# Graph attention on one Trainium2 core: own chunks ahead of shared rows, scatters eight steps behind, no writes behind gathers, and a wait for the score product three chunks ahead

## The chip, the cores and the metric

The kernel runs on one core of a Trainium2 chip. A core has five engines that each work off their own queue in order: TensorE (PE, with its weight loads shown apart as PEld), VectorE (DVE), ScalarE (ACT), GpSimd (POOL) and SyncE (SP). They hand work to each other through semaphores. Sixteen DMA engines move data between the chip's memory and the core's SBUF; POOL, ACT and SP issue the transfers. The metric is the device time of one execution in microseconds. Before the change it is 3419.34 us, the median of three runs (3416.0 to 3419.94).

## What is computed

Two layers of graph attention on 6250 nodes and 100000 edges, with 128 features in 8 heads of 16. Nodes have one of 16 types, edges one of 32. The core of a layer in the reference:

```
k = typed_linear(x, ntype, Wk).reshape(n, H, HS)     # also q and v
kT = jnp.einsum('nhd,htdo->nhto', k, Watt)           # a key for each node and edge type
vT = jnp.einsum('nhd,htdo->nhto', v, Wmsg)           # a value for each node and edge type
a = jnp.einsum('ehd,ehd->eh', kT[src, :, etype], q[dst]) * pri[:, etype].T / SQRT_D
att = edge_softmax(a, dst, n)
hag = segment_sum(vT[src, :, etype] * att, dst)
h = silu(typed_linear(hag, ntype, Wa))
h = h * alpha + x * (1.0 - alpha)
return layernorm(h) * g + b
```

After two layers follow a linear map, a residual and a layer norm.

## The kernel before

**Tables.** For each layer a table in the chip's memory holds one row of 256 numbers (key and value) for each pair of node and edge type, 200000 rows. The table of layer 0 is made in a first stage. The table of layer 1 is made during layer 0: as soon as a group of nodes has its new features, `table_block` (line 262) multiplies them on PE, ACT copies the result from PSUM into a tile `st` of 2 MB (line 281), and POOL scatters the tile into the table (`scatter`, line 1555). There are three `st` buffers (`STB`, line 1063). A node block of 128 nodes gives two tiles, so 49 blocks give 98 scatters.

**Blocks, slots and chunks.** Nodes are sorted by type class and degree into 49 blocks of 128, one node to a partition. Block b has `KB[b]` slots, as many as its largest degree. For each slot POOL issues one indirect DMA (line 1324) that gathers 128 rows of the table, 128 KB. Slots go in chunks of `CH` = 4; a chunk shares one `kv` tile, of which there are 12. A layer has 819 gathers in 224 chunks. When a chunk's rows have landed, DVE multiplies the keys by the query (line 1344, the score product) and sums over each head (line 1350).

**The end of a block.** When all scores of a block are there, the generator `finished` (line 1189) runs, one step at a time, between the chunks of the next block: mask, maximum, exponential on ACT (line 1213), denominator (line 1219), then chunk by chunk the values are weighted (line 1247) and added up (line 1254), and summed (line 1257). A `kv` tile is free again after its weighting and adding. In layer 0 the sum `acc` is in SBUF, in layer 1 it is in PSUM, in the first half of the tile `pair`.

**Shared rows.** One block, `TOP`, holds nodes with up to 42 edges. It has 26 own slots and 2 shared rows: a node with more than 26 edges gets rows of other partitions, and `moved` (line 1180) carries scores and values between partitions by a PE product and an ACT copy. It is handled once per layer. Before the change, `finished` deals with the shared rows (lines 1221 to 1237) ahead of the own chunks (lines 1243 to 1256).

**What sets the order.** POOL's order is that of the program text. For the other engines a planner orders the instructions by the text's order and by when it expects them to be ready; so a changed wait or a removed instruction can change their order too. Node work (`nodes`, line 1426) and table pieces are spread over the chunks by `tick` (line 1140). A finished `st` tile is put on the list `late` with a count (line 1579), each step of the table work lowers the counts (`later`, line 1548), and at zero the scatter is issued. A layer-1 gather waits for all scatters.

**Writes behind gathers.** After every gather POOL writes two pieces of 32 numbers per partition into a tile `pause` that nobody reads (lines 1327 to 1330).

Of the kernel before, what the change touches and what calls it, by code (L numbers as in the profile page):

```python
# [9 lines left out]
F32 = mybir.dt.float32  # L10
BF16 = mybir.dt.bfloat16
I32 = mybir.dt.int32
AF = mybir.ActivationFunctionType
ALU = mybir.AluOpType
# [4 lines left out]
P = 128  # L19
# [6 lines left out]
SB = 4  # L26
# [4 lines left out]

CH = 4

PAUSES = 12


PIECE = 6
# [34 lines left out]
def kernel(  # L72
# [21 lines left out]
    nc = tc.nc  # L94
    N, D = out.shape
# [5 lines left out]
    _, H, RT, HS, _ = Watt.shape  # L101
# [250 lines left out]
    half = wide // 2  # L352
# [43 lines left out]
    for i0 in range(0, NT, 17):  # L396
        sl = slice(i0, min(i0 + 17, NT))
        k = sl.stop - sl.start
# [173 lines left out]
    with tc.If(unsorted > 0):  # L572
# [7 lines left out]
        with tc.For_i(0, EC, 1) as j:  # L580
            pair = pp.tile([P, 2], I32, name="pair")
# [476 lines left out]
    def arm(fast):  # L1058
# [5 lines left out]
        ep = ctx2.enter_context(tc.tile_pool(name="ep", bufs=2))  # L1064
# [62 lines left out]
        def edges(l):  # L1127
# [61 lines left out]
            def finished(s, i, chunks, kvt, a, pair, sums, den):  # L1189


                i0, k, _ = sbs[s]
                K = KB[i0 + i]
                av = a[:, :K, :]
                rest = None
                if i0 + i == TOP:
                    rest, chunks = kvt[-1], chunks[:-1]
                    moved(pair, node_of, rest[:, 3, :RK * REST * H],
                          a[:, OWN:K, :].rearrange("p k h -> p (k h)"))
                    yield  # L1200
                nc.vector.tensor_tensor(  # L1201
                    av, av, neg[:, NO[i0 + i]:NO[i0 + i] + K].unsqueeze(2)
                    .to_broadcast([P, K, H]), op=ALU.add)
                yield
                m = ep.tile([P, H], F32, name="m")
                nc.vector.tensor_reduce(m, av.rearrange("p k h -> p h k"), axis=AX.X, op=ALU.max)
                yield
                nc.vector.tensor_tensor(av, av, m.unsqueeze(1).to_broadcast([P, K, H]),  # L1208
                                        op=ALU.subtract)
                w = av  # L1210
                if l and rest is None:
                    w = pair[:, 1, D:D + K * H].rearrange("p (k h) -> p k h", h=H)
                nc.scalar.activation(w, av, AF.Exp)
                if rest is not None:
                    moved(pair, rows_of, a[:, OWN:K, :].rearrange("p k h -> p (k h)"),
                          rest[:, 3, :RK * REST * H])
                yield
                yield
                nc.vector.tensor_reduce(den[:, i, :], w.rearrange("p k h -> p h k"),
                                        axis=AX.X, op=ALU.add)  # L1220
                if rest is not None:

                    wk = rest[:, 3, :RK * REST * H].rearrange("p (r c) -> p r c", r=RK)
                    nc.vector.tensor_tensor(
                        wk, wk, nth.unsqueeze(2).to_broadcast([P, RK, REST * H]), op=ALU.mult)
                    wr = rest[:, 3, D:D + REST * H]
                    nc.vector.tensor_reduce(wr, wk.rearrange("p r c -> p c r"), axis=AX.X,
                                            op=ALU.add)
                    yield
                    v = rest[:, :REST, D:].rearrange("p k (h d) -> p k h d", h=H)  # L1230
                    nc.vector.tensor_tensor(
                        v, v, wr.rearrange("p (k h) -> p k h", h=H).unsqueeze(3)
                        .to_broadcast([P, REST, H, HS]), op=ALU.mult)
                    nc.vector.tensor_tensor(rest[:, 2, D:], rest[:, 0, D:], rest[:, 1, D:],
                                            op=ALU.add)
                    moved(pair, node_of, rest[:, 2, D:], rest[:, 2, :D])
                    yield

                if l == 0:
                    acc = ep.tile([P, CH, D], F32, name="acc", bufs=1)  # L1240
                else:
                    acc = pair[:, 0].rearrange("p (k c) -> p k c", k=CH)
                for j in range(len(chunks) + 1):
                    if j < len(chunks):
                        j0, j1 = chunks[j]
                        v = kvt[j][:, :j1 - j0, D:]
                        nc.vector.tensor_tensor(  # L1247
                            (v if j else acc).rearrange("p k (h d) -> p k h d", h=H),
                            v.rearrange("p k (h d) -> p k h d", h=H),
                            w[:, j0:j1, :].unsqueeze(3).to_broadcast([P, j1 - j0, H, HS]),  # L1250
                            op=ALU.mult)
                    if j > 1:
                        j0, j1 = chunks[j - 1]
                        nc.vector.tensor_tensor(acc[:, :j1 - j0], kvt[j - 1][:, :j1 - j0, D:],  # L1254
                                                acc[:, :j1 - j0], op=ALU.add)
                    yield
                nc.vector.tensor_reduce(sums[:, i, :], acc.rearrange("p k c -> p c k"),  # L1257
                                        axis=AX.X, op=ALU.add)
                if rest is not None:
                    nc.vector.tensor_tensor(sums[:, i, :], sums[:, i, :], rest[:, 2, :D],  # L1260
                                            op=ALU.add)
                if i == k - 1:
                    spread(work, nodes(l, *sbs[s], sums, den, *got[s][1:], lambda gen: table(s, gen)),
                           (36 if l else 27) + (len(sbs[s][2]) - TC) // 2 * (1 if l else 3),
                           pace(s + 1) * (1.0 if l or mixed(s) else 0.75))
# [17 lines left out]
                    tables[s] = gen  # L1283
                    spread(pieces, gen, 4, PIECE)

            pause = ep.tile([P, PAUSES, 2, SB * H], BF16, name="pause", bufs=1)
            before = iter(())
            q, pair = query(0, 0)
            for s, (i0, k, types) in enumerate(sbs):
# [7 lines left out]
                for i in range(k):  # L1297
                    b = i0 + i
# [3 lines left out]
                    chunks = [(j, min(j + CH, own)) for j in range(0, own, CH)]  # L1302
                    if b == TOP:
                        chunks.append((OWN, OWN + REST))
                    kvt = []
# [12 lines left out]
                    for j0, j1 in chunks:  # L1318
                        c = j1 - j0
                        kv = ep.tile([P, CH, 2 * D], F32, name="kv", bufs=12)  # L1320
                        kvt.append(kv)
                        for j in range(j0, j1):
                            at = KO[b] + j
                            get = nc.gpsimd.indirect_dma_start(  # L1324
                                out=kv[:, j - j0, :], out_offset=None, in_=tabs[l][:],
                                in_offset=bass.IndirectOffsetOnAxis(ap=ell[:, at:at + 1], axis=0))
                            if at % PAUSES == 0:
                                pause = ep.tile([P, PAUSES, 2, SB * H], BF16, name="pause", bufs=1)
                            for half in range(2):
                                nc.gpsimd.memset(pause[:, at % PAUSES, half], 0.0)  # L1330
                            if l == 1:
                                for put in puts:
                                    tc.add_manual_dep(
                                        get.ins, put.ins.name,
                                        mybir.DependencyInfo(mybir.DependencyClass.Sync,
                                                             mybir.DependencyReason.DATA),
                                        reason="rows of the table")
                                puts.clear()
                        kk = kv[:, :c, :D]
                        rest = b == TOP and j0 == OWN  # L1340
                        if rest:
                            moved(pair, rows_of, got[s][0][:, i, :], kv[:, 2, :D])
                        of = kv[:, 2, :D] if rest else q
                        nc.vector.tensor_tensor(  # L1344
                            kk, kk, of.unsqueeze(1).to_broadcast([P, c, D]), op=ALU.mult)
                        step()
                        tick(c / 3)
                        to = (kv[:, 3, D:D + c * H].rearrange("p (k h) -> p k h", h=H) if rest
# [3 lines left out]
                        if rest:  # L1352
# [4 lines left out]
                                op=ALU.mult)  # L1357
# [10 lines left out]
                    q, pair = then[0] if then else (None, None)  # L1368
# [177 lines left out]
        late = []  # L1546
# [21 lines left out]
        def pieces_of(i0, k, kT, vT, share):  # L1568

            def steps(gen):  # L1570

                for _ in gen:
                    for _ in range(2):
                        later()
                        yield

            for i in range(k):
                def store(tg, st, b=i0 + i):
                    late.append([5, (tg, st, b)])

                yield from steps(table_block(ep, tps, kT, vT, i, share, STB, store,
                                             2 if fast else 1))
            while late and not fast:
                later()
# [172 lines left out]
```

## Time and profile before

| | |
|---|---|
| median of the runs | 3419.34 us |
| the profiled execution | 3404.81 us |
| its span, first to last instruction | 3403.0 us |
| POOL busy | 2403.5 us, 71% |
| DVE busy | 1863.1 us, 55% |
| PE busy | 1674.7 us, 49% |
| ACT busy | 1035.7 us, 30% |
| mean DMA | 198 GB/s |

The profile is of one execution. It has stages: up to about 640 us the first table and the sorting, from 640 to 2045 us the gathers of layer 0 (with the making of table 1), to 2115 us the last scatters, to 3360 us the gathers of layer 1, and 43 us of an end. A share of busy time over the whole span is a mean over stages with different limits, so each stage is read by itself. In the timeline a row gives start, duration, engine, line, operation, what is written and read, and, in brackets, how long the engine was idle before and what ended that; "issue" means that no wait is seen.

### The profile page before, as it was taken

The page shows a single profiled execution, that of the slowest core. Times are in us where ns is not written, and L with a number is a line of the kernel's source. Part 1 is how long each engine was busy: PE and PEld are TensorE (multiplying, and loading weights), DVE is VectorE, ACT ScalarE, POOL GpSimd, SP SyncE. Part 2 cuts the span into 40 slices and gives each one's busy share as a digit, 9 for nine tenths or more (in the row PEclk, how much of TensorE's full clock was granted, in tenths as well). Part 3 has the DMA queues.
Part 4 walks back from the last instruction along what each step waited for, and adds up shares of the span by engine and source line. Part 5 has one row for each costly group of instructions (what it writes and reads, how often), then busy time and mean ns, then how long its engine had stood idle before and what let it go on. Part 6 is the DMA issues. An engine that isn't in the chain of part 4 may idle for free. (4 is left out here: it accounts for less than half of the span.)

```text
span 3403.0 us, 24779 instructions
## 1 busy us (share of the span) xinstructions
PE 1674.7 (49%) x5291; PEld 747.6 (22%) x5291; DVE 1863.1 (55%) x4307; ACT 1035.7 (30%) x1720; POOL 2403.5 (71%) x5400
## 2 busy tenths in 40 slices
PE   5899989403676757776686664011111132012112
PEld 2444434201232323232232222000100011001001
DVE  8626642156555576566565543456455565566554
ACT  2788755200334123423344443011100120012111
POOL 2233267588677886888878872888688788888884
PEclk8889876556677667887777776555555555555555
DMA  6899989833676466766677767333233333333331
GB/s 181 363 418 420 391 332 345 269 87 97 215 266 253 134 219 225 279 251 212 225 263 286 279 234 294 99 99 97 83 98 96 98 108 98 94 99 99 94 89 44
DMA packets 169096, 674.80 MB, mean 198 GB/s; under 512 B 52972, under 2 KB 83726, under 8 KB 143886
## 3 DMA queue, kind: packets, MB, share of 16 engines
q0 software_dynamic: 114144, 638.40, 52.5%
q1 hardware_dynamic: 38402, 27.55, 3.0%
q10 hardware_dynamic: 16384, 7.11, 0.9%
q14 instruction: 120, 0.98, 0.1%
q8 instruction: 46, 0.75, 0.1%
HBM read 248.64 MB, written 425.02 MB: 198 GB/s over the span
## 5 line engine op out<-in xcount | busy, mean ns | idle before, releaser
L1324 POOL DMA_INDIRECT kv<-tab,ell x1638 | 1647.1, 1006 | 358.8 <-issue 298.2
L281 ACT COPY st<-tb 128x512 f32<-128x512 f32 (+1 forms) x1108 | 744.3, 759 | 507.9 <-PE tb L274 296.7
L1344 DVE TENSOR_TENSOR kv<-kv,tb 128x512 f32<-128x512 f32 (+3 forms) x223 | 142.9, 641 | 480.5 <-DMA kv<-tab,ell 469.0
L259 PE MATMUL nb<-ident,hag 128*128 128x128 f32 x98 | 26.4, 408 | 744.6 <-DVE hag L1391 420.5
L1330 POOL MEMSET pause<- 128x32 bf16 x3276 | 336.5, 141 | 49.0 <-remote 28.1
L1024 POOL DMA_INDIRECT tab<-st,rows x98 | 100.7, 1028 | 279.4 <-ACT st L281 253.2
L274 PE MATMUL tb<-bdv,kvT 32*128 32x512 f32 x784 | 257.7, 787 | 64.1 <-ACT st L281 50.9
L274 PE MATMUL tb<-bdk,kvT 32*128 32x512 f32 x784 | 261.6, 814 | 48.7 <-ACT st L281 35.0
L1344 DVE TENSOR_TENSOR kv<-kv,q 128x512 f32<-128x512 f32 (+3 forms) x223 | 142.8, 643 | 260.0 <-DMA kv<-tab,ell 237.7
L1350 DVE TENSOR_REDUCE a<-kv 128x32 f32<-128x512 f32 (+2 forms) x446 | 282.1, 635 | 4.7 <-DVE a L1208 1.5
L274 PE MATMUL tb<-bdv,vT 32*128 32x512 f32 x784 | 276.3, 776 | 10.7 <-ACT st L281 7.9
L251 PE MATMUL nb<-xm,wa 128*128 128x512 f32 (+2 forms) x336 | 188.9, 721 | 130.9 <-DVE xm L237 79.9
L274 PE MATMUL tb<-bdk,kT 32*128 32x512 f32 x784 | 236.9, 795 | 5.0 <-DVE st L279 2.5
L237 DVE SCALAR_TENSOR_TENSOR xm<-ntb,nb 128x512 f32<-128x512 bf16 (+2 forms) x304 | 156.6, 562 | 144.0 <-remote 65.5
L1556 POOL DMA_INDIRECT tab<-st,row x98 | 106.7, 1089 | 167.6 <-ACT st L281 120.0
L259 PEld LDWEIGHTS nb<-ident,hag 128*128 128x128 f32 x98 | 16.0, 203 | 761.7 <-issue 564.4
L1503 PE MATMUL nb<-xm,wkqv 128*128 128x512 f32 (+2 forms) x312 | 148.6, 639 | 41.1 <-issue 23.4
L251 PE MATMUL nb<-xm,wq 128*128 128x384 f32 (+2 forms) x168 | 85.0, 655 | 153.1 <-DVE a L1201 91.3
L1177 ACT COPY tb<-hq 128x128 f32<-128x128 f32 x49 | 13.1, 269 | 478.7 <-DVE sums L1257 311.7
L259 PE MATMUL nb<-ident,hs 128*128 128x128 f32 x98 | 36.3, 457 | 208.6 <-DVE hs L1464 122.0
L251 PEld LDWEIGHTS nb<-xm,wa 128*128 128x128 f32 x336 | 87.4, 277 | 232.7 <-DVE xm L237 99.7
L274 PEld LDWEIGHTS tb<-bdv,vT 32*128 32x128 f32 x784 | 110.9, 219 | 117.6 <-ACT st L281 78.6
(337 smaller groups left out, 2742.7 us busy)
## 6 DMA issues: line engine op xcount, KB each, us to landing
kv<-tab,ell POOLq DMA_INDIRECT x1638
hr<-xrd SPq DMA_DIRECT2D x14, 256.0 KB
hqd<-hs SPq DMA_DIRECT2D x7, 512.0 KB
hq<-hqd SPq DMA_DIRECT2D x7, 512.0 KB
xrd<-xr POOLq DMA_DIRECT2D x10, 256.0 KB
hr<-xrd SPq DMA_DIRECT2D x10, 192.0 KB
hqd<-hs SPq DMA_DIRECT2D x5, 384.0 KB
hq<-hqd SPq DMA_DIRECT2D x5, 384.0 KB
```

The source lines that it names most:

```text
L237: nc.vector.scalar_tensor_tensor(xm[:, :n], ntb[:, :n], float(t), hT[:, :n], op0=ALU.is_equal, op1=ALU.mult)
L251: nc.tensor.matmul(ps[:, :n], w[:, t, :], xm[:, :n], start=(t == types[0]), stop=(t == types[-1]))
L259: nc.tensor.transpose(tr[:, i * P:(i + 1) * P], src_of(i), ident)
L274: nc.tensor.matmul(pt[:, b], yT[s, i * P:(i + 1) * P], bd[s, tt, :], start=True, stop=True)
L281: nc.scalar.copy(to, pt)
L1024: put = nc.gpsimd.indirect_dma_start(out=tabs[0].rearrange("(n t) c -> n (t c)", t=16), out_offset=bass.IndirectOffsetOnAxis(ap=rows1[:, t ...
L1324: get = nc.gpsimd.indirect_dma_start(out=kv[:, j - j0, :], out_offset=None, in_=tabs[l][:], in_offset=bass.IndirectOffsetOnAxis(ap=ell[:, ...
L1330: nc.gpsimd.memset(pause[:, at % PAUSES, half], 0.0)
L1344: nc.vector.tensor_tensor(kk, kk, of.unsqueeze(1).to_broadcast([P, c, D]), op=ALU.mult)
L1350: nc.vector.tensor_reduce(to, kk.rearrange("p k (h d) -> p k h d", h=H), axis=AX.X, op=ALU.add)
L1503: nc.tensor.matmul(ps[:, :n], wkqv[:, j, t, :], xm[:, :n], start=(t == types[0]), stop=(t == types[-1]))
L1556: put = nc.gpsimd.indirect_dma_start(out=tabs[1].rearrange("(n t) c -> n (t c)", t=16), out_offset=bass.IndirectOffsetOnAxis(ap=row2[:, tg ...
```

## The change

Four edits.

1. In `finished` the block of statements for the shared rows moves behind the loop over the own chunks. In layer 1 the block `TOP` then sums into an SBUF tile `acc` and no longer into PSUM.
2. The two `pause` writes behind each gather go.
3. The first gather of each chunk gets a wait: the score product of the chunk three before it, in the same layer, must be done (`AHEAD` = 3, `begun`).
4. A scatter is issued eight steps of the table work after its tile is complete and no longer five.

```diff
-PAUSES = 12
+AHEAD = 3
...
                 nc.vector.tensor_reduce(den[:, i, :], w.rearrange("p k h -> p h k"),
                                         axis=AX.X, op=ALU.add)
-                if rest is not None:
-
-                    wk = rest[:, 3, :RK * REST * H].rearrange("p (r c) -> p r c", r=RK)
...
-                    moved(pair, node_of, rest[:, 2, D:], rest[:, 2, :D])
-                    yield
-
-                if l == 0:
+                if l == 0 or rest is not None:
                     acc = ep.tile([P, CH, D], F32, name="acc", bufs=1)
                 else:
                     acc = pair[:, 0].rearrange("p (k c) -> p k c", k=CH)
...
                         nc.vector.tensor_tensor(acc[:, :j1 - j0], kvt[j - 1][:, :j1 - j0, D:],
                                                 acc[:, :j1 - j0], op=ALU.add)
                     yield
+                if rest is not None:
+
+                    wk = rest[:, 3, :RK * REST * H].rearrange("p (r c) -> p r c", r=RK)
+                    nc.vector.tensor_tensor(
+                        wk, wk, nth.unsqueeze(2).to_broadcast([P, RK, REST * H]), op=ALU.mult)
+                    wr = rest[:, 3, D:D + REST * H]
+                    nc.vector.tensor_reduce(wr, wk.rearrange("p r c -> p c r"), axis=AX.X,
+                                            op=ALU.add)
+                    yield
+                    v = rest[:, :REST, D:].rearrange("p k (h d) -> p k h d", h=H)
+                    nc.vector.tensor_tensor(
+                        v, v, wr.rearrange("p (k h) -> p k h", h=H).unsqueeze(3)
+                        .to_broadcast([P, REST, H, HS]), op=ALU.mult)
+                    nc.vector.tensor_tensor(rest[:, 2, D:], rest[:, 0, D:], rest[:, 1, D:],
+                                            op=ALU.add)
+                    moved(pair, node_of, rest[:, 2, D:], rest[:, 2, :D])
+                    yield
+
                 nc.vector.tensor_reduce(sums[:, i, :], acc.rearrange("p k c -> p c k"),
                                         axis=AX.X, op=ALU.add)
...
-            pause = ep.tile([P, PAUSES, 2, SB * H], BF16, name="pause", bufs=1)
+            begun = []
...
-                            if at % PAUSES == 0:
-                                pause = ep.tile([P, PAUSES, 2, SB * H], BF16, name="pause", bufs=1)
-                            for half in range(2):
-                                nc.gpsimd.memset(pause[:, at % PAUSES, half], 0.0)
+                            if j == j0 and len(begun) >= AHEAD:
+                                tc.add_manual_dep(
+                                    get.ins, begun[-AHEAD],
+                                    mybir.DependencyInfo(mybir.DependencyClass.Sync,
+                                                         mybir.DependencyReason.DATA),
+                                    reason="no further ahead of the scores")
...
-                        nc.vector.tensor_tensor(
-                            kk, kk, of.unsqueeze(1).to_broadcast([P, c, D]), op=ALU.mult)
+                        begun.append(nc.vector.tensor_tensor(
+                            kk, kk, of.unsqueeze(1).to_broadcast([P, c, D]), op=ALU.mult).ins.name)
...
                 def store(tg, st, b=i0 + i):
-                    late.append([5, (tg, st, b)])
+                    late.append([8, (tg, st, b)])
```

More of the change, by code (lines that the diff above doesn't have):

```diff
@@ L1220, in finished @@
                                         axis=AX.X, op=ALU.add)
-                if rest is not None:
-                    wk = rest[:, 3, :RK * REST * H].rearrange("p (r c) -> p r c", r=RK)
-                    nc.vector.tensor_tensor(
[L1225 to L1228, printed above, removed]
-                    yield
[L1230 to L1235, printed above, removed]
-                    moved(pair, node_of, rest[:, 2, D:], rest[:, 2, :D])
-                    yield
-                if l == 0:
+                if l == 0 or rest is not None:
                     acc = ep.tile([P, CH, D], F32, name="acc", bufs=1)
@@ L1343, in edges @@
                         of = kv[:, 2, :D] if rest else q
-                        nc.vector.tensor_tensor(
-                            kk, kk, of.unsqueeze(1).to_broadcast([P, c, D]), op=ALU.mult)
+                        begun.append(nc.vector.tensor_tensor(
+                            kk, kk, of.unsqueeze(1).to_broadcast([P, c, D]), op=ALU.mult).ins.name)
                         step()
```

## The prediction

> **What bounds the kernel now.** I read the table by stage first, then POOL's groups in the two gather stages, then the waits there, then the timeline at the places that the change touches. The rows by stage give the length, then busy time of PE, PEld, DVE, ACT and POOL, the granted clock, the DMA share and GB/s:
>
> ```profile
> 0.00:640.00 640.00, 552.66 (x2100) 260.53 (x2100) 321.33 (x797) 389.48 (x763) 267.15 (x339) 0.80 0.89 347
> 640.00:2045.00 1405.00, 869.04 (x2570) 357.54 (x2570) 799.14 (x1705) 470.72 (x625) 1124.22 (x2548) 0.71 0.63 221
> 2045.00:2115.00 70.00, 38.43 (x140) 18.31 (x140) 26.15 (x54) 24.55 (x31) 7.93 (x8) 0.70 0.79 317
> 2115.00:3360.00 1245.00, 204.75 (x457) 105.12 (x458) 696.37 (x1689) 141.96 (x287) 1000.21 (x2502) 0.54 0.33 97
> ```
>
> Layer 1 is POOL's stage: 1000 of 1245 us busy, PE at 205, DMA at a third. In layer 0 POOL has 1124 of 1405 us, but PE, at a clock of 0.71, has 869 and DVE 799, each in order. The groups of POOL, layer 0 then layer 1, with busy time, mean ns and idle time before:
>
> ```profile
> L1324 POOL DMA_INDIRECT kv<-tab,ell x819 | 860.0, 1050 | 163.9 <-issue 134.4 <-SPq L1753 14.7 <-DVE acc L1247 6.4
> L1330 POOL MEMSET pause<- 128x32 bf16 x1638 | 167.4, 142 | 3.4 <-remote 2.2 <-issue 0.5 <-POOL pause L1330 0.2
> L1556 POOL DMA_INDIRECT tab<-st,row x91 | 99.8, 1096 | 117.2 <-ACT st L281 89.5 <-issue 15.7 <-ACT a L1213 7.7
> ...
> L1324 POOL DMA_INDIRECT kv<-tab,ell x819 | 787.2, 961 | 194.9 <-issue 163.8 <-DVE tb L1247 19.2 <-DVE a L1350 1.0
> ```
>
> And who waits in layer 0, then in layer 1 (us in total, times, longest):
>
> ```profile
> DVE kv L1344 <- DMA kv<-tab,ell: 234.2, 80, 8.7
> POOL tab L1556 <- ACT st L281: 89.5, 20, 10.3
> ACT st L281 <- DMA tab<-st,row: 16.2, 5, 7.4
> ...
> DVE kv L1344 <- DMA kv<-tab,ell: 469.0, 157, 20.3
> POOL kv L1324 <- DVE tb L1247: 19.2, 1, 19.2
> ```
>
> In layer 1 DVE stands idle for rows 469 us and POOL for DVE hardly at all, so a quicker POOL is a shorter stage. In layer 0 DVE waits for rows 234 us and POOL waits for ACT 89.5 us: it is mixed.
>
> **The pause writes go.** 336 us of busy time are not 336 us of path, as the distance from one gather to the next shows, with the writes and (a loop without them, early in the kernel) without:
>
> ```profile
> 2629.62 0.95 POOL L1324 DMA_INDIRECT kv<-tab,ell  x1 [0.15 <-issue]
> 2630.57 0.21 POOL L1330 MEMSET pause<- 128x32 bf16 x2
> 2630.93 0.95 POOL L1324 DMA_INDIRECT kv<-tab,ell  x1 [0.15 <-issue]
> ...
> 44.24 0.95 POOL L968 DMA_INDIRECT xg<-in_x_dram,inv  x1 [0.30 <-issue]
> 45.49 0.95 POOL L968 DMA_INDIRECT xg<-in_x_dram,inv  x1 [0.30 <-issue]
> ```
>
> With them 1.31 us (0.95 + 0.21 + 0.15), without 1.25 (0.95 + 0.30): the writes fill a gap that is there anyway, and 0.06 us remains. 819 x 0.06 = 49 us per layer. In layer 1 I count all of it; what is late next is the gather again. In layer 0 I also count 49, and book separately what the other engines take back.
>
> **Own chunks first.** The 19.2 us in layer 1 are the block behind `TOP`: its fifth chunk is the thirteenth tile and needs the first tile of `TOP`, whose weighting stands behind the shared rows:
>
> ```profile
> 2451.80 0.76 DVE L1219 TENSOR_REDUCE den<-a 128x8 f32<-128x336 f32 x1 [0.61 <-ACT a L1213]
> ...
> 2463.35 0.70 DVE L1247 TENSOR_TENSOR tb<-kv,a 128x512 f32<-128x512 f32 x1 [0.92 <-ACT kv L1187]
> ...
> 2464.32 0.95 POOL L1324 DMA_INDIRECT kv<-tab,ell  x1 [19.24 <-DVE tb L1247]
> ```
>
> Moved, the first weighting can follow the denominator at 2452.6 and ends at 2453.3: 11 us come off, 8 of the 19 stay. (From 0, if the planner leaves it late, to 19.) In layer 0 this weighting already ran at once, into SBUF, so 0 there. The price is the SBUF `acc` of layer 1: gathers beside adds of two SBUF tiles are slower, 1050 against 961 ns on average above. 0.089 x 819 over 49 blocks is 1.5 us a block, some 4 us for the large one. The Trainium skill, "SBUF — State Buffer", section "Who interferes with whom", says that a VectorE tensor_tensor with two SBUF inputs holds up only what GpSimd reads, and infers that descriptor generation, which writes, is not hurt; by that these 4 us would be 0. The rows disagree with the inference.
>
> **Scatters three steps later.** A step of table work falls on 1.5 gather slots (4 steps to `PIECE` = 6 slots), so three are 4.5 slots, 5.6 us at 1.25. Per scatter nothing is added: the same 98 by about 1.1 us, past four or five gathers, which then go ahead of it. 20 waits of 4.5 us on average, 10.3 at most, shrink by up to 5.6 each: I take 75 of the 89.5 us (0 to 89.5). The cost is on the other side. Eight steps are two tiles, so scatter n now is issued just ahead of the first copy into its buffer's next use. How near that is already:
>
> ```profile
> 1798.97 1.38 POOL L1556 DMA_INDIRECT tab<-st,row  x1 [0.16 <-issue]
> ...
> 1807.10 1.93 ACT L281 COPY st<-tb 128x1024 f32<-128x1024 f32 x2 [0.73 <-DMA tab<-st,row]
> ```
>
> From issue to free it takes 8.1 us. The Trainium skill, "DMA: Bandwidth & Descriptors", section "Anatomy of one DMA — SWDGE (gpsimd) path", gives 2.0 us plus bytes at 436 GB/s; my estimate from it for 2 MB is 6.8 us, which would make this cost a little smaller; the row decides. Behind the waiting copy stand on ACT the exponential that DVE needs and PE's next table products. ACT waits so 16.2 us today. I take +10 us on the path (0 to 134, the rival below).
>
> **The new wait.** In step, DVE's product ends about 2.7 us after a chunk's last gather, while POOL issues two more chunks, 10 us, before the wait matters; so DVE must be over 7 us late. What queues behind a waiting gather on POOL: all later gathers, scatters and output writes; DVE waits for the first. In layer 1 DVE is the one that waits, and I take 10 us (0 to 20). In layer 0 it is late at three places; the gather shown opens its chunk, the DVE row is the product three chunks ahead of it:
>
> ```profile
> 666.81 0.95 POOL L1324 DMA_INDIRECT kv<-tab,ell  x1 [0.15 <-issue]
> 678.55 1.29 DVE L1344 TENSOR_TENSOR kv<-kv,q 128x512 f32<-128x512 f32 x2
> ...
> 1117.95 0.95 POOL L1324 DMA_INDIRECT kv<-tab,ell  x1 [0.15 <-issue]
> 1139.27 0.89 DVE L1344 TENSOR_TENSOR kv<-kv,q 128x512 f32<-128x512 f32 x2
> 1149.61 1.16 POOL L1324 DMA_INDIRECT kv<-tab,ell  x1 [6.36 <-DVE acc L1247]
> ...
> 2011.29 0.97 POOL L1324 DMA_INDIRECT kv<-tab,ell  x1 [0.30 <-issue]
> 2021.40 0.69 DVE L1344 TENSOR_TENSOR kv<-kv,q 128x512 f32<-128x512 f32 x1
> ```
>
> 12.4 us at the start, 22.0 less the 6.4 that the twelve tiles cost anyway, and 10.8 near the end: 39 us. A POOL that gains 124 us over this layer meets DVE's late places oftener, since those come from PE and do not move; I take 95 us, between 39 and 140, where all of layer 0's gain is lost. The wait itself is on the engine for which the tile wait exists already, so no instruction is added.
>
> **What no row shows** is how the planner orders DVE, ACT and PE after this. I take 0; its bounds are the rivals.
>
> **The sum.** Layer 1: -49 - 11 + 4 + 10 = -46. Layer 0: -49 - 75 + 10 + 95 = -19. First stage, the 70 us between the layers and the end: 0. Together -65 us, on the profiled execution 3404.8 to 3340. The runs' median is 14.5 us above that execution, so 3354.
>
> **The rivals.**
> (a) The new wait is dear: every late chunk pays its whole lateness and DVE never catches up. Over the rows of the two lines 31 of the 224 chunks of layer 0 start ahead of the end of the product three before, from the one at 666.81 above to the layer's last:
>
> ```profile
> 2041.77 0.68 DVE L1344 TENSOR_TENSOR kv<-kv,q 128x512 f32<-128x512 f32 x1
> 2042.33 0.97 POOL L1324 DMA_INDIRECT kv<-tab,ell  x1 [0.30 <-issue]
> ```
>
> Their lateness adds to 244 us. With 244 for 95 the time is 3354 + 149 = 3503. It decides against the change above 160 us. For it: PE and DVE are near POOL in layer 0, and a re-planned DVE queue acts alike. Against: after each late place DVE stands waiting for rows again, 234 us in sum.
> (b) The tiles are reused too late. Scatter n and the first copy into tile n+3 make 95 pairs, the first and the last of them:
>
> ```profile
> 868.92 1.31 POOL L1556 DMA_INDIRECT tab<-st,row  x1 [6.65 <-ACT st L281]
> 883.30 1.93 ACT L281 COPY st<-tb 128x1024 f32<-128x1024 f32 x2 [6.27 <-PE tb L274]
> ...
> 2091.02 0.97 POOL L1556 DMA_INDIRECT tab<-st,row  x1 [18.80 <-ACT st L281]
> 2098.12 1.93 ACT L281 COPY st<-tb 128x1024 f32<-128x1024 f32 x2 [3.07 <-DMA tab<-st,row]
> ```
>
> In 24 of the 95 the copy starts less than 13.7 us (8.1 + 5.6) after the scatter and would be held up by up to 5.6: 134 us of ACT waits at most. If half of it reaches PE and so the tiles, the scatters find them as late as today: 60 more and the 75 not gained, 3354 + 135 = 3489. For it: PE's products and ACT's copies wait on each other in order. Against: the median pair has 21 us.
> (c) The wait costs only 39 us and all 89.5 us of scatter waits go: 3354 - 56 - 14 = 3284. For it: POOL is busiest in both layers.
> (d) The gains in POOL are eaten in layer 0 and the wait binds in layer 1: no change, 3419.
>
> **How the numbers follow.** Forecast 0.50, (a) 0.18, (b) 0.14, (c) 0.12, (d) 0.06. The forecast is near -65 and its own bounds reach from 3300 to 3410. Of the slower cases I leave out the dear half: the range is 3285 to 3480. A change under 0.2% (7 us) can't be told from none here; faster 0.62, same 0.06, slower 0.32.
>
> **What would show it.** In layer 1 gathers 1.25 us apart and the stage near 1200 us; a wait of about 8 us behind `TOP`. In layer 0 POOL waiting for `DVE kv L1344`, some 95 us, few waits on `ACT st`, `ACT st <- DMA tab` up from 16 us. Wrong it is if POOL's waits for the product pass 160 us, or layer 0 grows beyond 1405 us, or gathers without the writes are not 1.25 us apart.

## The result, and the profile after

Beside each other on one chip the kernel before took 3415.14 us and the kernel after 3439.57 us (medians). The ratio is 1.0072, with a 95% interval of 1.0054 to 1.0090: slower by 0.7%, where 3354 us was forecast. Later pairs, on two chips, gave 1.0074 [1.0046, 1.0101] and 1.0119 [1.0085, 1.0154]. The profiled execution took 3440.0 us.

First lines and two rows of the groups of the page of after (idle time and its releasers stand behind the bar):

```profile
span 3437.9 us, 21524 instructions
PE 1698.0 (49%) x5291; PEld 756.1 (22%) x5291; DVE 1874.3 (55%) x4307; ACT 1037.3 (30%) x1720; POOL 2049.7 (60%) x2124
L1324 POOL DMA_INDIRECT kv<-tab,ell x1638 | 1626.0, 993 | 749.6 <-issue 460.6
L1558 POOL DMA_INDIRECT tab<-st,row x98 | 106.3, 1085 | 212.5 <-ACT st L281 166.6
```

POOL works 354 us less than before, and the kernel is longer. The windows of after, from the first gather of a layer to its last product (window, length, busy time and instructions of PE, PEld, DVE, ACT, POOL, then PE's granted clock, DMA share and GB/s):

```profile
650.00:2067.00 1417.00, 879.93 (x2548) 362.26 (x2550) 801.61 (x1703) 467.35 (x621) 937.91 (x908) 0.68 0.62 216
2137.00:3394.00 1257.00, 207.63 (x455) 106.71 (x456) 703.14 (x1687) 140.29 (x280) 830.41 (x864) 0.53 0.33 95
```

Layer 0 of before, cut in the same way:

```profile
651.00:2050.00 1399.00, 869.22 (x2572) 357.72 (x2574) 799.68 (x1708) 471.96 (x627) 1125.18 (x2548) 0.71 0.63 220
```

Against 1399 and 1245 us before, layer 0 grew by 18 us and layer 1 by 12. The gathers do come 1.25 us apart; the median distance in layer 1 is 1.254 us against 1.312. Layer 1 had to shrink by that, and grew. The timeline of DVE in after shows what took its place:

```profile
2812.89 0.29 DVE L1422 BATCH_NORM_STATS2 bn<-hs 128x6 f32<-128x128 f32 x1 [0.91 <-DVE hs L1455]
2814.29 0.29 DVE L1422 BATCH_NORM_STATS2 bn<-hs 128x6 f32<-128x128 f32 x1 [1.10 <-DVE bn L1422]
2815.00 0.29 DVE L1422 BATCH_NORM_STATS2 bn<-hs 128x6 f32<-128x128 f32 x1 [0.42 <-issue]
2817.09 0.18 DVE L1425 BATCH_NORM_AGGREGATE mv<-bn 128x2 f32<-128x6 f32 x1 [1.79 <-remote]
2818.50 0.18 DVE L1425 BATCH_NORM_AGGREGATE mv<-bn 128x2 f32<-128x6 f32 x1 [1.23 <-DVE mv L1425]
2819.89 0.18 DVE L1425 BATCH_NORM_AGGREGATE mv<-bn 128x2 f32<-128x6 f32 x1 [1.21 <-DVE mv L1425]
```

Six short instructions that need nothing but DVE's own results take 7 us for 1.4 us of work. Each waits for a semaphore of DVE alone, whose instruction had ended. The distances of the starts are 1.40, 0.71, 2.09, 1.41 and 1.39 us, close to multiples of 0.70 us. I call such an instruction a late start: idle over 0.25 us ahead of a DVE instruction that waits for DVE's own semaphore only. The groups of layer 1, first before and then after, say that most of it is new:

```profile
L1254 DVE TENSOR_TENSOR tb<-kv,tb 128x512 f32<-128x512 f32 (+3 forms) x166 | 104.8, 631 | 0.5 <-DVE kv L1344 0.3
L1420 DVE BATCH_NORM_STATS2 bn<-hs 128x6 f32<-128x128 f32 x47 | 10.6, 279 | 0.0
L1423 DVE BATCH_NORM_AGGREGATE mv<-bn 128x2 f32<-128x6 f32 x92 | 9.4, 157 | 2.4 <-DVE mv L1423 2.1 <-DVE bn L1420 0.3
```

```profile
L1236 DVE TENSOR_TENSOR tb<-kv,tb 128x512 f32<-128x512 f32 (+3 forms) x160 | 101.0, 631 | 53.1 <-remote 32.6 <-issue 10.8 <-DVE a L1352 4.6
L1422 DVE BATCH_NORM_STATS2 bn<-hs 128x6 f32<-128x128 f32 x47 | 12.6, 288 | 26.6 <-DVE bn L1422 14.9 <-remote 8.1 <-DVE hs L1455 2.7
L1425 DVE BATCH_NORM_AGGREGATE mv<-bn 128x2 f32<-128x6 f32 x92 | 10.4, 160 | 23.9 <-DVE mv L1425 11.0 <-remote 7.3 <-issue 3.0
```

The durations hardly move (631 and 631 ns), the idle time ahead of them does: 0.5 to 53.1, 0.0 to 26.6, 2.4 to 23.9 us. Added over all of DVE's rows in layer 1, late starts go from 24 us (25 of them) to 247 us (155), while the other idle times over 0.25 us fall from 534 to 318 us. That closes the account of layer 1: -216 + 223, and 7 us more busy time, make 14 us; the stage grew by 12. What DVE no longer waits for rows and other engines, it waits for itself. Layer 0 is not explained by this (below).

### The profile page after: what moved, and what is told of

Its sections match the earlier page's. It is cut to its first block, busy times and chain, and to the rows that moved or that the text cites. A ratio compares the mean times of both kernels' runs of the same rounds, so it can differ in the third digit from the quotient of the medians.

```text
span 3437.9 us, 21524 instructions
## 1 busy us (share of the span) xinstructions
PE 1698.0 (49%) x5291; PEld 756.1 (22%) x5291; DVE 1874.3 (55%) x4307; ACT 1037.3 (30%) x1720; POOL 2049.7 (60%) x2124
## 5 line engine op out<-in xcount | busy, mean ns | idle before, releaser
L1324 POOL DMA_INDIRECT kv<-tab,ell x1638 | 1626.0, 993 | 749.6 <-issue 460.6
L259 PE MATMUL nb<-ident,hag 128*128 128x128 f32 x98 | 26.6, 411 | 747.1 <-DVE hag L1393 397.4
L274 PE MATMUL tb<-bdk,kvT 32*128 32x512 f32 x784 | 254.5, 844 | 87.4 <-ACT st L281 70.3
L1236 DVE TENSOR_TENSOR tb<-kv,tb 128x512 f32<-128x512 f32 (+3 forms) x168 | 105.7, 629 | 53.2 <-remote 32.6
L251 PE MATMUL nb<-xm,wq 128*128 128x384 f32 (+2 forms) x168 | 95.0, 721 | 66.5 <-DVE xm L237 48.4
```

The costliest lines, as they stand in the source:

```text
L251: nc.tensor.matmul(ps[:, :n], w[:, t, :], xm[:, :n], start=(t == types[0]), stop=(t == types[-1]))
L259: nc.tensor.transpose(tr[:, i * P:(i + 1) * P], src_of(i), ident)
L274: nc.tensor.matmul(pt[:, b], yT[s, i * P:(i + 1) * P], bd[s, tt, :], start=True, stop=True)
L1324: get = nc.gpsimd.indirect_dma_start(out=kv[:, j - j0, :], out_offset=None, in_=tabs[l][:], in_offset=bass.IndirectOffsetOnAxis(ap=ell[:, ...
```

## The experiments

The kernel before ran beside each group of kernels, on the same chip. The chips were not all alike. On three of them the kernel before took 3410 to 3412 us (below: a slower chip), on two 3222 us (a faster chip). Only ratios on one chip are compared. Each chip ran one group only, so "chip" means the chip with whatever else was particular to that group. "Late" is the sum of late starts in layer 1 of one profiled execution.

| kernel | slower chips: ratio [95%] | late, us | faster chips: ratio [95%] | late, us |
|---|---|---|---|---|
| before | 1 | 24 | 1 | not profiled |
| no_pause | 1.0306 [1.0275, 1.0337], 1.0280 [1.0240, 1.0320] | 355, 361 | | |
| wait3 | 1.0016 [0.9998, 1.0034] | 29 | | |
| late8 | 1.0013 [0.9993, 1.0033] | 37 | | |
| own_first | 0.9983 [0.9959, 1.0007] | 22 | | |
| after_2, after_3 | 1.0074, 1.0119 | 267, 255 | | |
| after_writes | 0.9969 [0.9945, 0.9993] | 24 | 0.9918 [0.9902, 0.9933] | 0 |
| no_pause_wait | | | 0.9769 [0.9747, 0.9790] | 0 |
| one_write | 1.0140 [1.0096, 1.0184] | 136 | 0.9792 [0.9773, 0.9811] | 0 |
| wide_write | 1.0072 [1.0043, 1.0102] | 104 | 0.9868 [0.9851, 0.9885] | 0 |
| chunk_write | | | 0.9798 [0.9779, 0.9817] | 0 |
| three_writes | | | 1.0256 [1.0239, 1.0272] | 0 |
| two_ahead | 1.0088 [1.0052, 1.0125] | 189 | 0.9786 [0.9770, 0.9802] | 0 |

**Each edit alone.** Theory: the gathers gain as forecast and the new wait eats it. Rivals: the writes were needed; or the other engines' order changes.

no_pause, the kernel before without the writes:

```diff
-                            for half in range(2):
-                                nc.gpsimd.memset(pause[:, at % PAUSES, half], 0.0)
```

> The kernel before without the two writes behind each gather, the other three edits left out. Theory 1 (the wait eats the gain): the gathers come 1.25 us apart with nothing lost elsewhere, so about 50 us less in layer 1 and 30 to 60 less in layer 0, some 3320 to 3350 us. Theory 2 (the writes are needed): DVE's stalls between its own instructions, 24 us of layer 1 before and 247 after, come with the denser gathers; then they show here too, over 150 us in layer 1, and the time is 3415 to 3445. Theory 3 (the other engines' order): the time falls by 20 to 60 us and the stalls don't show.

wait3, with the wait and the writes:

```diff
+                            if j == j0 and len(begun) >= AHEAD:
+                                tc.add_manual_dep(get.ins, begun[-AHEAD], ...)
```

> The kernel before with only the wait for the score product three chunks ahead; writes kept. Theory 1: POOL waits for the product in both layers and the time grows by 40 to 100 us, to 3455 to 3515, with over 60 us of POOL's waits at the product. Theory 2: gathers 1.31 us apart leave DVE on time; the wait costs the 39 us of the three late places in layer 0 at most, 3415 to 3455, and DVE's stalls in layer 1 stay near 24 us. Theory 3: DVE's stalls in layer 1 go up here, because the wait has another order of DVE's work planned.

late8:

```diff
-                    late.append([5, (tg, st, b)])
+                    late.append([8, (tg, st, b)])
```

> The kernel before with the scatters eight steps behind and no longer five. By the prediction's step POOL's waits at scatters for the copy into their tile fall from 89.5 us to about 15 in layer 0 and the time falls by 50 to 75 us, to 3345 to 3370. Rival: the tile is then reused too late, ACT waits for the scatter, the products and so the next tiles come later, and POOL's scatter waits stay as they were (120 us in the kernel after): no change, or up to 20 us more.

own_first moves the block of the shared rows behind the loop over the own chunks and sums `TOP` into SBUF in layer 1, as in the change:

> The kernel before with only the own chunks ahead of the shared rows. By the prediction's step 11 of the 19.2 us behind the large block in layer 1 go and 4 are added: 7 us less, 3405 to 3415. Rival (order): the planner gives the other engines another order around the large block, and the time moves by 10 us or more either way.

The measured ratios settle it for the second theory. The removal of the writes, the largest term of the forecast gain, costs 3% alone, and the wait alone costs nothing that can be told from zero. The loss is dearer than that theory had it: 3515 us for 3415 to 3445, so the other edits take some of it back. The timeline of no_pause shows a long late start:

```profile
2457.80 0.95 POOL L1323 DMA_INDIRECT kv<-tab,ell  x1 [0.30 <-issue]
...
2461.19 0.69 DVE L1257 TENSOR_REDUCE sums<-tb 128x128 f32<-128x512 f32 x1 [5.47 <-remote]
2463.30 0.16 DVE L1405 TENSOR_TENSOR t<-t,v 128x4 f32<-128x4 f32 x1 [1.42 <-DVE sums L1257]
2463.38 0.32 DVE L1206 TENSOR_REDUCE m<-a 128x8 f32<-128x96 f32 x1
2463.99 0.27 ACT L1177 COPY tb<-hq 128x128 f32<-128x128 f32 x1 [8.68 <-DVE m L1206]
```

DVE stands 5.47 us ahead of a reduction whose operands are its own. POOL's last gather ended at 2458.75 (2457.80 + 0.95), and POOL runs nothing more until 2478.82: the first 3 us of the 5.47 fall beside gathers, the rest and the next 1.42 us don't. So a gather in progress on POOL is not needed for it. ACT's row names DVE's `m`, which ended at 2463.70, and ACT starts 0.29 us after that: not only DVE sees DVE's results late. The Trainium skill, "SBUF — State Buffer", section "Who interferes with whom", holds that the port pair shared with GpSimd is the only cause of contention between engines, and that a tensor_reduce on trn2 never contends. These late starts strike reductions too, and the rows above show one beside which POOL was idle in part, so by that page's own rule the port is not their cause.

In no_pause late starts in layer 1 add 331 us to the kernel before and DVE's other idle times fall by 283: 48 us, and 10 us more busy time, against 58 us by which the layer grew (1303 for 1245). That is little more than half of the loss. Layer 0 grew by 63 us in no_pause and by 36 in no_pause_2, with 46 and 50 us of late starts in it (none in before). What else lengthens layer 0 was not isolated, and single executions differ there: the profiled execution of late8, the longest of its twelve, has 32 us more than before in layer 0 without one late start, while its median is that of before.

late8 was to shorten POOL's waits at scatters. Rows of the waits in layer 0, late8:

```profile
POOL tab L1556 <- ACT st L281: 122.0, 28, 13.6
```

89.5 us in 20 waits became 122.0 in 28. The distance from a tile's last copy to its scatter did not grow by 5.6 us; its median fell from 6.0 to 3.6 us. When the last copy of a tile ends, POOL has issued 5.5 gathers more than before (mean of 96 tiles), and the scatter stands 4.4 gathers later. In this execution POOL used the slack to run ahead and met the table work again. In after_writes_2 below, also with eight steps, these waits are 57 us, but there POOL waits 65 us for the product.

own_first did what was forecast. The first gather that found no tile behind `TOP`, in layer 1 of own_first:

```profile
2457.43 1.16 POOL L1324 DMA_INDIRECT kv<-tab,ell  x1 [8.62 <-DVE acc L1229]
...
2466.47 0.68 DVE L1236 TENSOR_TENSOR acc<-kv,acc 128x512 f32<-128x512 f32 x1
2466.81 3.30 POOL L1324 DMA_INDIRECT kv<-tab,ell  x1 [0.15 <-issue]
```

19.24 us became 8.62. The last row is the price: a gather of 3.30 us while DVE weights and adds in SBUF back to back. In layer 1 of before, where sums are in PSUM, no gather takes over 1.5 us. The nine gathers beside these sums take 2.6 us more than nine of 0.955, the median. The ratio is worth -6 us, and its interval reaches past zero.

wait3's direct price, from the waits of the whole execution:

```profile
POOL kv L1326 <- DVE kv L1352: 44.6, 18, 11.4
```

**The change with writes, and the kernel with fewer writes.** after_writes is the kernel after with the two writes put back. no_pause_wait has no writes and the wait, without the other two edits.

> The kernel after with the two writes behind each gather put back. Theory 2 (the missing writes alone make the loss): the other three edits together are worth what they gave alone, +0.16, +0.13 and -0.17% of the kernel before, so 3405 to 3425 and DVE's stalls in layer 1 back below 40 us. Rival (the edits interact, the planned order of all four is bad): it stays above 3430.

> No writes, and the wait three chunks ahead; scatters at five steps and shared rows first as before. Theory 2 with the wait as a remedy: the wait keeps POOL from running dense and takes back some 75 us of the 103 that the missing writes cost, so 3430 to 3450, with 150 to 280 us of DVE's stalls in layer 1. Rival: the remedy lies in the other two edits; then it is 3480 to 3520 like the kernel without writes.

one_write and chunk_write are the kernel before with fewer writes:

```diff
-                            for half in range(2):
+                            for half in range(1):
...
-                            for half in range(2):
+                            for half in range(2 if j == j0 else 0):
```

> The kernel before with one write behind each gather in place of two. If any write between two gathers keeps DVE on time: gathers some 1.25 to 1.28 us apart, DVE's stalls under 60 us in layer 1, and the time falls by 20 to 40 us, to 3370 to 3395. If the distance of the gathers decides: part of the loss of the kernel without writes, stalls of 100 to 300 us in layer 1, 3425 to 3500.

> Two writes behind the first gather of a chunk alone, 448 in place of 1638 pairs of the kernel before. If one write now and then is enough to let DVE through, the stalls end within a chunk: under 100 us in layer 1, and the time is 3370 to 3415. If every dense pair of gathers harms, the stalls stay above 200 us and the time is 3460 to 3515.

These four ran on a faster chip. None has a single late start, and everything that takes writes away gains 2%. The expected times were for a chip on which before takes 3412 us; that chips could differ had been missed. What they had said of the distance holds there. Layer 1 of after_writes, and then of no_pause_wait, on that chip:

```profile
2000.00:3146.00 1146.00, 198.47 (x454) 104.49 (x455) 691.78 (x1687) 141.91 (x287) 999.06 (x2502) 0.54 0.36 105
```

```profile
1998.00:3100.00 1102.00, 197.07 (x454) 103.93 (x455) 691.36 (x1687) 141.91 (x287) 825.43 (x864) 0.54 0.38 109
```

44 us less in layer 1, for gathers 1.252 and no longer 1.309 us apart (0.057 x 819 = 47). The two kernels also differ in the scatters and the shared rows.

**Chip or edit.** The kernel after, no_pause, one_write and after_writes, unchanged, once more:

> The kernel after, unchanged, once more, beside the kernel before on the same chip. The two sets of runs so far were on two chips, on which the kernel before takes 3412 and 3222 us. If the loss belongs to a chip (DVE's late starts between its own instructions were 24 to 355 us in layer 1 on the first and 0 in all four kernels on the second): on a chip like the second the kernel after is 1 to 2.5% faster than before, without late starts; on one like the first it is again 0.5 to 1% slower, with 200 us or more of them. If the loss belongs to the edits, it is slower on both.

> The kernel before without the writes, once more. On a chip like the second: no late starts, gathers 1.25 us apart, 1.5 to 2.5% faster. On one like the first: 3% slower as before.

> One write behind each gather, once more. On a chip like the second: 2% faster as there. On one like the first: with late starts that follow the distance of the gathers, 25 to 200 us of them in layer 1 and a time between that with two writes (0) and with none (+3%).

> The kernel after with its writes put back, once more. On a chip like the second: 0.8% faster than before as there. On one like the first: the sum of the three other edits alone, +0.1%, and DVE's late starts below 40 us in layer 1.

This was a slower chip, and all four went much as expected of one: late starts back, 3% and 0.7% lost without writes. The kernel after with its writes gained 0.3%, where +0.1% was expected. So the same source, one_write, is 2.1% faster than before on one chip and 1.4% slower on another. One group of DVE, the adding of weighted values in PSUM, shows it over the whole execution. On the slower chips no_pause, no_pause_2, one_write_2 and then, on the faster one, no_pause_wait:

```profile
L1254 DVE TENSOR_TENSOR tb<-kv,tb 128x512 f32<-128x512 f32 (+3 forms) x174 | 109.9, 632 | 79.2 <-remote 42.2 <-issue 12.4 <-DVE kv L1339 11.8
```

```profile
L1254 DVE TENSOR_TENSOR tb<-kv,tb 128x512 f32<-128x512 f32 (+3 forms) x174 | 109.8, 631 | 71.8 <-remote 37.2 <-issue 15.7 <-DVE a L1345 10.5
```

```profile
L1254 DVE TENSOR_TENSOR tb<-kv,tb 128x512 f32<-128x512 f32 (+3 forms) x174 | 109.4, 629 | 15.1 <-remote 7.2 <-DVE kv L1344 2.0 <-DVE rd L1384 1.4
```

```profile
L1255 DVE TENSOR_TENSOR tb<-kv,tb 128x512 f32<-128x512 f32 (+3 forms) x174 | 109.1, 627 | 0.1
```

Same work, same durations, idle ahead of it 79.2, 71.8, 15.1 and 0.1 us.

The packed traces also hold the times at which updates of semaphores were recorded, and they part the chips without exception. On the faster ones 4020 to 4049 updates of DVE's semaphore are recorded, one for each of the 4021 to 4048 instructions that make one; in no_pause_wait the median comes 11 ns after the instruction's end. On the slower ones it is 2756 (before) to 3064 (no_pause) for as many instructions, and over all semaphores 16000 to 18600 against 43800 to 44200 on the faster chips. Updates are late there: 433 of the 3064 in no_pause come over 60 ns after the last end, against 2 of 4027 in no_pause_wait. Of the 211 late starts in layer 1 of no_pause 166 follow such a record of DVE's semaphore within 60 ns. As far as these records show, then, the update comes late and DVE starts at once on it. Whether missing updates were merged or only not recorded can't be told; before lacks the most of DVE's, with few late starts. All times on record are of executions that the profiler recorded, so it is not shown either that the late updates occur without it.

The late starts do not account for all of the loss with one write. In one_write_2, and in wide_write_2 below, layer 1 is about as long as before (1243 and 1248 us): there the late starts eat what the gathers gain. Layer 0 is 36 and 38 us longer, with 1 and 2 us of late starts.

**Number or length of the writes, and a tighter wait.**

```diff
-                            for half in range(2):
-                                nc.gpsimd.memset(pause[:, at % PAUSES, half], 0.0)
+                            nc.gpsimd.memset(pause[:, at % PAUSES], 0.0)
...
+                            for half in range(3):
...
-AHEAD = 3
+AHEAD = 2
```

The first is wide_write, the second three_writes (with tiles of eight gathers in place of twelve), the third two_ahead, made from the kernel after.

> One write of 64 numbers behind each gather in place of two of 32. If the number of instructions that POOL runs between two gathers keeps DVE on time: as with one write of 32, 100 to 170 us of late starts in layer 1 and +1 to +1.8% on a chip where the kernel before takes 3410. If the length of the writing does it: under 50 us, and within 0.5% of the kernel before. On a chip where it takes 3220: like one write there, 1.5 to 2.2% faster.

> Three writes behind each gather in place of two, tiles of eight gathers in place of twelve. By number: on a chip where the kernel before takes some 3410 us DVE's late starts in layer 1 go 361, 136, 24 us with none, one and two writes, so with three they are under 10, while the gathers come 1.37 us apart, some 50 us more a layer at most: 3420 to 3480. By distance it would be the same with any spacing. On a chip where the kernel before takes some 3220 us there are no late starts and it is only the distance that counts: 1.5 to 3% slower.

> The kernel after with the wait two chunks ahead in place of three. If the wait helps because it keeps POOL from issuing gathers while DVE is late, the tighter wait takes back more on a chip where the kernel before takes 3410: late starts under 200 us in layer 1 and 3400 to 3430. Rival: with two chunks POOL stands at each chunk of four, because the rows are on their way longer than that, and the time is 3450 to 3560 there, and 3200 to 3300 where the kernel before takes 3220.

They fell on a faster chip, where there is nothing to repair: three writes cost 2.6%, the other two gain 1.3 (1.5 to 2.2 was expected) and 2.1%. Two of them and the kernel after were then run once more:

> One write of 64 numbers in place of two of 32, once more; where the kernel before took 3222 us it was 1.3% faster. On a chip where the kernel before takes 3410: if the number of POOL's instructions between gathers decides, 100 to 170 us of late starts in layer 1 and +1 to +1.8%; if the length does, under 50 us and within 0.5%.

> The kernel after with the wait two chunks ahead, once more; where the kernel before took 3222 us it was 2.1% faster. On a chip where the kernel before takes 3410: late starts under 200 us in layer 1 and 3400 to 3430 if the wait helps by holding POOL while DVE is late; 3440 and more with over 230 us if it doesn't.

> The kernel after, unchanged. On a chip where the kernel before takes 3222 us, on which it has not run: no late starts and 1.5 to 2.5% faster, like its neighbours there (the wait two chunks ahead -2.1%, no writes and the wait alone -2.3%). On a chip where the kernel before takes 3410: 0.5 to 1% slower as twice before.

On this slower chip one write of 64 numbers leaves 104 us of late starts. One write of 32 left 136 on another slower chip, two of 32 leave 22 to 37 in five executions. So most of it seems to hang on the number of writes; three writes never ran on a slower chip. Whether length has a part stays open: the late starts are near those of one write, but 1.0072 is under the 1 to 1.8% expected by number. One write of 32 had 1.0140 on another chip, where the kernel after was the quicker one (1.0074 for 1.0119). The distance of the gathers as such is an unlikely cause: from none to one write of 32 it grows by 6 ns (1.251 to 1.257 us, medians of layer 1), and late starts go from 361 to 136 us; from there it grows by 28 ns to the write of 64 (1.285), and they go to 104. The tighter wait has fewer late starts (189 for 255 on the same chip), but its 0.9% loss can't be told from the 1.2% of after_3, so neither expectation held whole. POOL's waits for the product double. Of two_ahead_2, beside 92.3 us in 37 waits of after and 79.7 in 30 of after_3:

```profile
POOL kv L1324 <- DVE kv L1346: 208.2, 71, 17.3
```

No run tells why late starts are fewer with the tighter wait, nor what in the slower chips makes them. The kernel after itself never ran on a faster chip; two_ahead, which differs from it in the wait alone, gained 2.1% there.

## Why the prediction was wrong

**"pause writes go" is the step that failed.** Its distance was right: 1.25 us, and 44 of the forecast 49 us in layer 1 between two kernels on a chip without late starts. Its silent term, that nothing else changes when POOL's writes go, was wrong on the slower chips. -98 us was forecast for the two layers, and no_pause measured +2.8 and +3.1%, 96 to 104 us: a term mis-sized by some 200 us. What the runs show in its place are late starts of DVE, 24 us of layer 1 with the writes and 355 and 361 without; they more than eat the 49 us there, and in layer 0 a loss of 36 to 63 us stands whose cause is shown only in part. That 3439.57 lies inside the range of 3285 to 3480 is luck: its slow part stood for rivals (a) and (b), and neither came. The profile of before held 24 us of late starts in layer 1; they look like noise there. A quantity that is small with the writes in place says nothing of its size without them, and no range was set for it.

**Own chunks first.** The stall of 19.2 us was to fall to 8; it fell to 8.62. Net -7 was forecast, -6 measured, in a measurement of about as much. The SBUF sum cost 2.6 us for the 4 forecast, so the rows were rightly taken over a price of 0.

**Scatters.** -75 + 10 was forecast; the ratio was +0.13%, about +4 us. The step failed where it held ACT's copies fixed and let only POOL move. POOL was 5.5 gathers further on when a tile's last copy ended, so it reached the scatter sooner behind that copy and not later. That the table work sets the pace there is a reading of this and not shown by itself. The other side, a tile reused too late, did not come either: ACT's waits for a scatter in layer 0 fell from 16.2 us to 1.9 in after (row below).

**The new wait.** Its price beside the writes was forecast at 10 + 95 us. With the writes the waits are 35 us in layer 0, near the 39 of the three places quoted, and 9 in layer 1, and the ratio was +0.16%, 12 us at most by its interval. The 95 were meant for denser gathers; layer 0 of after has 54 us of these waits and that of no_pause_wait, on the faster chip, 17, so they were too many. In layer 1 of after it is 39 for 10. The kernel after is 0.7 to 1.2% slower where the missing writes alone cost 3%, so some of the other three edits are worth something without the writes. That it is the wait is likely, but no_pause_wait never ran on a slower chip.

**The planner's order, taken as 0.** With the writes in place all three other edits give 0.9969 on a slower chip, -10 us; alone they add to +0.12%. And one program in one order, one_write, gains on one chip and loses on another. So a bad order is not what makes the loss; that the order without writes costs nothing is not shown.

**The rivals.** Rival (a), a late DVE that POOL must wait for, came nearest in sign, but its place and cause were others: it was to start in layer 0 from PE's late results and cost 149 us. Of the three signs named for a wrong prediction one came: layer 0 grew beyond 1405 us, to 1417. Its 18 us are less well explained than layer 1. Late starts of DVE there are 25 us, and POOL's waits at scatters rose (the waits of after in layer 0):

```profile
POOL tab L1558 <- ACT st L281: 130.1, 30, 9.3
...
ACT st L281 <- DMA tab<-st,row: 1.9, 1, 1.9
```

The first row is 40.6 us more than before, and late8 alone shows 32.5 of that at no cost in its median. What the 18 us are stays open. In after_2 and after_3 they are 31 and 28, but wait3 and late8 have 19 and 32 us more too in their profiled executions, at ratios that can't be told from 1.

**The version to keep.** On the slower chips that is after_writes, 0.9969 [0.9945, 0.9993], and it is faster than before on the faster chip too, 0.9918. Where late starts don't occur, no_pause_wait has the lowest ratio that was measured, 0.9769, and one_write, chunk_write and two_ahead are within 0.3% of it.

## What to carry to other kernels

An instruction whose result nobody reads can still matter to other engines: before it is costed as its own time, the engines around it are to be looked at with and without it. When idle time moves from "waits for data" to "waits for its own last instruction" at unchanged durations, the stage is not limited by what the edit made faster. And a tuned filler is to be measured on more than one chip, since the same source was here 2.1% faster on one and 1.4% slower on another.

## What was not expected of the hardware

- DVE's instructions that wait for DVE's own semaphore can start late, by up to 6.8 us (no_pause, layer 1), at distances near multiples of 0.70 us, while instructions without a wait don't: none of 412 in layer 1 of no_pause had over 0.25 us of idle time ahead of it, against 211 of 765 that wait for DVE alone. With two small writes of POOL behind each gather there are 22 to 37 us of it in layer 1, without any 355 and 361.
- POOL's own writes start late on those chips too. Layer 1 of after_writes on the faster and then on a slower chip:

```profile
L1332 POOL MEMSET pause<- 128x32 bf16 x1638 | 166.6, 141 | 0.4
```

```profile
L1332 POOL MEMSET pause<- 128x32 bf16 x1638 | 167.4, 140 | 50.5 <-remote 32.9 <-issue 14.4 <-POOL pause L1332 0.8
```

  Equal durations, 0.4 and 50.5 us of idle time.
- On the slower chips a third or so of DVE's semaphore updates are not in the trace (2756 of 4045 in before), on the faster ones none is missing (4027 for 4026 in no_pause_wait), and late starts follow late updates.
- A gather that takes 0.95 us otherwise took 3.30 us beside DVE's weighting and adding in SBUF (own_first, layer 1).
- Chips differ by 6% for the same kernel (3222 and 3412 us for before). The gathers' own durations don't (963 and 960 ns a gather in layer 1 of after_writes). In the first stage of after_writes PE is busy for 515.7 us on the faster and 551.1 on the slower chip, at granted clocks of 0.81 and 0.80:

```profile
0.00:636.00 636.00, 515.68 (x2100) 250.84 (x2100) 321.17 (x799) 384.78 (x763) 266.89 (x339) 0.81 0.91 355
```

```profile
0.00:647.00 647.00, 551.05 (x2100) 258.74 (x2100) 321.49 (x799) 389.54 (x763) 266.89 (x339) 0.80 0.89 349
```

- The first write behind a gather costs the distance 6 ns (1.251 to 1.257 us), the second 52 ns (to 1.309).
